# Masked attention with residual: the second batch's rows fetched later, its queries moved up, a slot formula with fewer dependent steps

## The chip, the core and the metric

The kernel runs on one core of one Trainium2 chip. The metric is the device time of one execution in microseconds (us); three timed runs gave 977.62, 977.0 and 977.0, a median of 977.0. A profiled execution of the same program took 974.4 us, of which the profile's span, from the first to the last instruction, is 972.7.

The core has engines that run side by side, each through its own instructions in order: TensorE (PE for matmuls, PEld for its weight loads), VectorE (DVE), ScalarE (ACT), GpSimd (POOL) and SyncE (SP). They wait for each other through semaphores. Transfers are issued by SP (plain ones) and POOL (gathers and scatters by an index) and carried by 16 DMA engines.

## The reference

16 sequences of 1024 tokens with 512 features and a 0/1 mask per token; 8 heads of 64. The query, the key and the value are all the same projection:

```python
xt = jnp.transpose(x, (0, 2, 1))
q = xt @ Wq.T
qh = q.reshape(B, T, NH, dk).transpose(0, 2, 1, 3)
scores = scale * jnp.einsum('bhqd,bhkd->bhqk', qh, qh)
cmask = mask[:, None, None, :]
rmask = mask[:, None, :, None]
logits = (scores * cmask + (1.0 - cmask) * NEG) * rmask
attn = jax.nn.softmax(logits, axis=-1)
ctx = jnp.einsum('bhqk,bhkd->bhqd', attn, qh)
ctx = ctx.transpose(0, 2, 1, 3).reshape(B, T, D)
out = ctx @ Wo.T
return x + jnp.transpose(out, (0, 2, 1))
```

A masked token's own row of logits is all zero, so its result is the same for all masked tokens of a sequence: the mean of q over all tokens. An active token attends to the active tokens of its sequence only.

## The kernel before

The kernel packs the active tokens. A token's **slot** is its rank among the active ones if it is active, and otherwise the number of active ones plus its rank among the others. The first 512, 528 or 544 slots of a batch (one batch is one sequence) are the ones that attention is computed for; batch 0 has 512, batch 1 has 544.

Start. `order` counts the active tokens per batch (eight matmuls) and ranks the batches by it; "batch 0" is a place in this order. `permute` picks a place's mask, `sources` finds which batch of the input it is: `base` (the number of its first row in `x_in`) and `first_row`, an integer in memory that SP reads (`source`, a register load) before it can address the batch's own features in `x_nat_in`. `slots` (line 244) gets the ranks `pr` by eight matmuls of the mask against a triangle and against ones, the total `pn` by eight more, and makes the slot from them on DVE; then the slot's number of 128 (`hi`) and place in it (`lo`). `hot` makes a one-hot table of `lo`, `index` turns it by eight small matmuls into `idx`, the row numbers in slot order. `gather` then fetches 128 rows (256 KB) at a time, by POOL. `warm(n)` issues n matmuls of 128x512 on constants, which compute nothing that is used, so that TensorE is kept busy.

Each gathered chunk is transposed on TensorE (`xt`), and split into an upper and a lower 16-bit part `xh`, `xl` (`xsplit`: ACT, then DVE). `query(b, e, g)` projects one of four 128-feature blocks e, one half g of the slots, by twelve matmuls. ACT copies the result to `q`, DVE zeroes what lies past the active tokens (`hr`), and `qsplit` makes `hl`, from which SP's four transfers per e spread `xx`, the operands of `scores`. `value` transposes q (batch 0) or multiplies xx by a constant (the others).

The mean. A batch's features are loaded once more, whole and untransposed (`load_half`: 256 KB, `load_all`: 512 KB), and summed along the tokens: on ACT (`sum_half`, a copy with an accumulator), or for the last four halves of batch 1 on DVE (line 462). The mean goes as an extra column behind the slots of `xh`, `xl` and through `query`; `mq` is what comes out. `extra` says which batch carries another's mean in column A + 1 (A slots) beside its own in column A: before, batch 1 carries batch 0's. `load_all` uses the buffers `xm`, of which there are two; batch 1's halves use those, `ub`, and four of `xi`.

Then come the batches one after the other (`run`, from line 1179). A batch has 18 slots of the plan, four per pair of heads p and two more. In a slot TensorE computes one group of `scores` for two blocks of keys; ACT takes four exponentials of it (line 793); `attend` (line 813) multiplies an earlier pair's exponentials with the values. Between these, `plan[(slot, half)]` puts the other work by hand: the transposes, queries and values of the next batch n, the index and gathers of the batch after that, the rest of the last batch's. `free[slot]` holds loads and sums. TensorE's order in this part is exactly the order in which the program issues; the other engines' orders are decided by a scheduler with priorities (`high_priority`) and fixed in the compiled program. `behind(i)` puts instructions behind instruction i in that order, and the argument `after` of a load makes the transfer wait for an instruction.

The lines that the change touches in this plan: the start from line 1099 on (`slots(0, 1)`, `warm(9)`, `hot(0)`), the loads at line 1128, `half1` (line 1140), batch 0's own plan at line 1233, and the loads of later batches at line 1259.

## Time and profile before

| | before |
|---|---|
| median of three timed runs | 977.0 us |
| profiled execution, whole | 974.4 us |
| its span | 972.7 us |
| TensorE, busy in the span | 936.1 us, 96% |
| VectorE | 718.3 us, 74% |
| ScalarE | 648.6 us, 67% |
| GpSimd | 304.8 us, 31% |
| mean granted TensorE clock | 0.996 |

A row of the profile in order of time has the start in us from the span's start, the duration, the engine, the line, the operation, what it writes and reads by the program's names, the shape, and how many in a row. What stands in brackets is the engine's idle time just before and what ended it. A table by stretches gives for each stretch its length, every engine's busy time with the number of instructions, the granted clock (1.00 is full), the mean busy share of the DMA engines and GB/s.

### The profile page before, as it was taken

How to read it: one execution, taken by the hardware profiler on the slowest of the kernel's cores; microseconds unless marked ns; L12 is line 12 of the kernel's file. 1: busy time of each engine (PE TensorE's matmuls, PEld its weight loads, DVE VectorE, ACT ScalarE, POOL GpSimd, SP SyncE). 2: the span in 40 equal slices, each digit the busy share in tenths (PEclk: the TensorE clock that was granted, in tenths of full speed). 3: DMA queues.
4: the chain of work that ended last, by engine and by line, in shares of the span. 5: the costliest groups of instructions: out<-in, count | busy, mean ns of one | idle time of the engine just before them, and what ended most of it. 6: DMA issues, size and time to landing. Idle time of an engine off the chain costs nothing.

```text
span 972.7 us, 22828 instructions
## 1 busy us (share of the span) xinstructions
PE 936.1 (96%) x8124; PEld 582.3 (60%) x8124; DVE 718.3 (74%) x2441; ACT 648.6 (67%) x1677; POOL 304.8 (31%) x309
## 2 busy tenths in 40 slices
PE   7788999999999999999999999999999999999997
PEld 4455656656666666666666666666666666565543
DVE  7767867777776777877687777886777788785563
ACT  5766766667667676676767678666767766565651
POOL 2101013033250432505234240332505135243452
PEclk9999999999999999999999999999999999999999
DMA  8736455557565676756657677655657857555552
GB/s 253 211 99 171 136 164 160 160 179 213 166 191 165 179 216 188 214 144 200 184 178 225 192 231 223 188 155 142 198 172 239 235 151 211 144 163 161 168 179 101
DMA packets 79144, 176.30 MB, mean 181 GB/s; under 512 B 14544, under 2 KB 22480, under 8 KB 79024
## 3 DMA queue, kind: packets, MB, share of 16 engines
q1 hardware_dynamic: 57968, 107.09, 39.2%
q0 software_dynamic: 21056, 67.68, 22.4%
q8 instruction: 66, 1.08, 0.5%
q14 instruction: 54, 0.44, 0.2%
HBM read 91.36 MB, written 33.91 MB: 129 GB/s over the span
## 4 chain that ended last, share of the span: by engine, by line
PE 82%; DVE 7%; DMA 4%; ACT 4%; issue 2%; SPq 1%; POOL 0%; POOLq 0%; DVEq 0%; ACTq 0%
PE pss L813 21%; PE pss L778 17%; PE pm L937 17%; PE pm L552 16%; ACT p L793 2%; PE pss L831 2%; DMA xx<-hl 2%; PE pm L524 2%; PE pss L724 1%; DMA xa<-x_in,idx 1%; PE pm L615 1%; DVE xl L483 1%; PE pss L937 1%; DVE xa L943 1%; PE pm L867 1%
## 5 line engine op out<-in xcount | busy, mean ns | idle before, releaser
L793 ACT ACTIVATE p<-pss,nm 128x528 f32<-128x528 f32 (+2 forms) x512 | 354.4, 703 | 103.5 <-PE pss L778 96.3
L813 PE MATMUL pss<-p,v 128*64 128x264 f32 (+2 forms) x2048 | 243.0, 390 | 0.0
L778 PE MATMUL pss<-xx 128*128 128x118 f16 (+17 forms) x1856 | 214.7, 289 | 3.6 <-ACT p L793 2.0
L1006 POOL DMA_INDIRECT y_out<-xa,idx x68 | 81.9, 1205 | 409.0 <-DVE nq L690 84.8
L813 PEld LDWEIGHTS pss<-p,v 128*64 128x64 f32 x2048 | 141.6, 137 | 86.1 <-issue 5.8
L778 PEld LDWEIGHTS <-xx 128*128 128x128 f16 (+1 forms) x1856 | 103.4, 96 | 85.0 <-issue 35.1
L552 PE MATMUL pm<-xh,wqh 128*128 128x264 f16 (+5 forms) x512 | 141.9, 277 | 3.7 <-DVE xl L483 1.8
L552 PE MATMUL pm<-xh,wql 128*128 128x264 f16 (+5 forms) x512 | 141.3, 276 | 0.0
L552 PE MATMUL pm<-xl,wqh 128*128 128x264 f16 (+5 forms) x512 | 141.1, 276 | 0.0
L552 PEld LDWEIGHTS <-wqh 128*128 128x128 f16 x1024 | 96.4, 97 | 33.0 <-issue 14.1
L422 POOL DMA_INDIRECT xa<-x_in,idx x68 | 72.8, 1071 | 127.8 <-DMA y_out<-xa,idx 43.7
L793 ACT ACTIVATION_READ_ACCUMULATOR p<-pss,nm 128x1 f32 x512 | 105.2, 205 | 0.0
L937 PE MATMUL pm<-woh,ch 128*128 128x512 f16 x240 | 91.1, 380 | 0.0
L937 PE MATMUL pm<-woh,cl 128*128 128x512 f16 x240 | 90.9, 379 | 0.0
L937 PE MATMUL pm<-wol,ch 128*128 128x512 f16 x240 | 90.9, 379 | 0.0
L556 ACT ACTIVATE q<-pm 128x264 f32<-128x264 f32 (+5 forms) x128 | 50.9, 397 | 44.2 <-PE pm L552 44.0
L619 ACT COPY v<-pm 128x512 f32<-128x512 f32 x64 | 37.5, 586 | 59.8 <-PE pm L615 56.6
L1006 POOL DMA_INDIRECT y_out<-xi,idx x60 | 64.3, 1071 | 36.6 <-PE pss L724 16.8
L943 DVE SCALAR_TENSOR_TENSOR xa<-pm,xa 128x512 f32<-128x512 f32 x61 | 41.6, 682 | 46.1 <-PE pm L937 45.6
L937 PEld LDWEIGHTS <-ch 128*128 128x128 f16 x480 | 44.8, 98 | 47.5 <-issue 4.1
L422 POOL DMA_INDIRECT xi<-x_in,idx x60 | 59.6, 993 | 21.2 <-issue 15.8
L836 ACT COPY c<-pss 128x528 f32<-128x528 f32 (+2 forms) x64 | 38.3, 598 | 41.9 <-PE pss L831 26.4
(231 smaller groups left out, 1489.1 us busy)
## 6 DMA issues: line engine op xcount, KB each, us to landing
xm<-x_nat_in SPq DMA_DIRECT2D x56, 512.0 KB
xx<-hl SPq DMA_DIRECT2D x208, 136.0 KB
rb<-rd SPq DMA_DIRECT2D x72, 132.0 KB
xx<-hl SPq DMA_DIRECT2D x48, 128.0 KB
pt<-c SPq DMA_DIRECT2D x36, 132.0 KB
pt<-p SPq DMA_DIRECT2D x36, 132.0 KB
rb<-rd SPq DMA_DIRECT2D x32, 136.0 KB
ub<-ud SPq DMA_DIRECT2D x16, 256.0 KB
```

Source lines behind the costliest of these rows:

```text
L422: dma = self.nc.gpsimd.indirect_dma_start(out=tile[:n], out_offset=None, in_=self.x, in_offset=bass.IndirectOffsetOnAxis(ap=idx, axis=0))
L524: self.pe = nc.tensor.transpose(pt[:, c, :], x[:n, c * P:(c + 1) * P], self.ident[:n, :n]).ins
L552: self.beat = nc.tensor.matmul(pq, lhsT=w[:, c, e * P:(e + 1) * P], rhs=xx[:, c, cols], start=(k == 0), stop=(k == 3 * DC - 1)).ins
L556: nc.scalar.activation(s["q"][:, e, cols], pq, AF.Copy, scale=1.0 / (SX * SW))
L619: nc.scalar.copy(v, pv)
L778: m = nc.tensor.matmul(flat[:, c0:c1], lhsT=w, rhs=x, start=banks[n] not in banks[:n], stop=banks[n] not in banks[n + 1:])
L793: e = nc.scalar.activation(t, flat[:, at:at + A], AF.Exp, bias=s["nm"][p // 2][:, p % 2 * 2 + k:p % 2 * 2 + k + 1], scale=SCALE, accum_out ...
L813: mm = nc.tensor.matmul(pav[k * DK:(k + 1) * DK, g], lhsT=s["v"][p][:, i, k * DK:(k + 1) * DK], rhs=ps[k, i][:, cols], start=(i == 3), sto ...
L836: self.context_out = nc.scalar.copy(c[:, :A].rearrange("p (g c) -> p g c", g=2), pav).ins
L937: mm = nc.tensor.matmul(po[:cols.stop - cols.start], lhsT=a[:, e, cols], rhs=w[:, e, :], start=(e == 0 and k == 0), stop=(e == DC - 1 and ...
L943: return self.nc.vector.scalar_tensor_tensor(x, po, 1.0 / (SX * SW), x, ALU.mult, ALU.add).ins
L1006: dma = self.nc.gpsimd.indirect_dma_start(out=self.out, out_offset=bass.IndirectOffsetOnAxis(ap=idx, axis=0), in_=x, in_offset=None)
```

## The change

The slots of batch 0 and of batch 1 come from a new function, `slots_of`; the other batches keep `slots`. With m the mask, it makes 1 - m, 2m - 1 and (token number) x (1 - m) from the mask alone, counts the total first and the ranks second, and takes slot = (2m - 1) x rank + (1 - m) x total + token number x (1 - m). The comparison table `kk_kept` holds 544 in place of 640 as its fifth bound, so that the shift of slots past 544 needs one operation.

```diff
+        for k, first in ((0, P), (4, C)):
+            nc.gpsimd.iota(self.kk_kept[:, k:k + 4], pattern=[[P, 4]], base=first, ...)
...
+        nc.vector.tensor_scalar(free, mb, -1.0, 1.0, ALU.mult, ALU.add)
+        nc.vector.tensor_scalar(sign, mb, 2.0, -1.0, ALU.mult, ALU.add)
+        nc.vector.tensor_tensor(put, self.tok, free, ALU.mult)
...
+        nc.vector.tensor_copy(n, pn)
+        nc.vector.scalar_tensor_tensor(base, free, n, put, ALU.mult, ALU.add)
+        nc.vector.tensor_tensor(slot, sign, pr, ALU.mult)
+        nc.vector.tensor_tensor(slot, slot, base, ALU.add)
+        nc.vector.tensor_tensor(ge, slot..., self.kk_kept..., ALU.is_ge)
+        nc.vector.scalar_tensor_tensor(far, ge[:, :, 4], float(5 * P - C), slot, ALU.mult, ALU.add)
+        nc.vector.tensor_reduce(hi, ge, AX.X, ALU.add)
+        nc.vector.scalar_tensor_tensor(self.lo[:, b], hi, -float(P), far, ALU.mult, ALU.add)
...
-            self.sources(0, 2)
-            self.slots(0, 1)
-        self.warm(9)
-        self.hot(0)
+            self.slots_of(0)
+            self.hot(0)
+            self.sources(0, 2)
+        self.warm(6)
```

The last four half loads of batch 0 are issued behind the third transposed chunk and not the first. Batch 1's eight half loads go; its features come as four whole loads in batch 0's slots 5, 8, 11 and 14, between batch 2's, all through the two `xm` buffers, each summed on ACT two slots after its load (batch 2's were summed four slots after). Its mean is carried by batch 2 and not by batch 1.

```diff
-            if k == 0:
+            if k == 2:
                 for i in range(DC, 2 * DC):
                     self.load_half(0, i, self.pe)
-                for i in range(DC):
-                    self.load_half(1, i, self.pe)
...
-        self.extra = {1: 0, B - 5: B - 4, B - 2: B - 1}
+        self.extra = {1: 0, 2: 1, B - 5: B - 4, B - 2: B - 1}
...
-                        at = 3 * c + (k if b else 4)
+                        at = 3 * c + k + (0 if b else 4)
...
-                if b == 0:
-                    for k in range(2 * DC):
-                        if k >= DC:
-                            free.setdefault(0, []).append(lambda k=k: half1(k))
-                        free.setdefault(3 + k // 2, []).append(L(self.sum_half, 1, k))
```

Batch 0's plan (x: transposes of batch 1, q(e, g): its queries, v: values, tv, tc: tails, pre, post, hot, index, take: mask, slots, one-hot table, index and gathers for batch 2 on):

```diff
-                                (3, 0): query(0, 3, 1) + value(0, 3) + pk(b, 1) + x[:1],
-                                (5, 0): x[1:2], (5, 1): x[2:3],
-                                (7, 0): x[3:] + tp(b, 1) + q(0, 0) + bt(b, 1), (8, 1): pre,
-                                (9, 0): q(0, 1), (9, 1): q(1, 0) + post, (11, 0): hot,
-                                (12, 0): q(1, 1) + tc(0) + v(0) + rng[:2], (12, 1): index, (13, 0): take[:3],
-                                (14, 0): tv(0) + q(2, 0) + rng[2:], (14, 1): v(1) + q(2, 1) + pk(n, 0),
-                                (16, 0): q(3, 0) + tp(n, 0) + take[3:], (16, 1): q(3, 1),
-                                (17, 0): bt(n, 0) + v(2) + tc(1) + [(0, L(self.means, n))]}
+                                (3, 0): query(0, 3, 1) + x[:1] + value(0, 3) + pk(b, 1), (4, 0): x[1:2],
+                                (5, 0): x[2:3], (5, 1): x[3:],
+                                (7, 0): tp(b, 1) + q(0, 0) + bt(b, 1) + q(0, 1), (8, 1): pre + q(1, 0),
+                                (9, 1): post, (11, 0): hot + q(1, 1),
+                                (12, 0): tc(0) + v(0) + rng[:2] + q(2, 0), (13, 1): index,
+                                (14, 0): tv(0) + q(2, 1) + rng[2:] + take[:3], (14, 1): v(1) + q(3, 0) + pk(n, 0),
+                                (16, 0): q(3, 1) + tp(n, 0) + take[3:], (16, 1): bt(n, 0),
+                                (17, 0): v(2) + tc(1) + [(0, L(self.means, n))]}
```

More of the change, by code (lines that the diff above doesn't have):

```diff
@@ L117, in setup @@
         self.kk = iota("kk", [P, NB - 1], [[P, NB - 1]], P, 0)
+        self.kk_kept = fixed("kk_kept", [P, NB - 1])
+        for k, first in ((0, P), (4, C)):
+            nc.gpsimd.iota(self.kk_kept[:, k:k + 4], pattern=[[P, 4]], base=first, channel_multiplier=0,
+                           allow_small_or_imprecise_dtypes=True)
         self.ionb = iota("ionb", [P, NB], [[1, NB]], 0, 0)
@@ L280, in slots, with slots_of @@
                                     self.tok.unsqueeze(2).broadcast_to([P, TB, NB]), ALU.mult)
+    def slots_of(self, b):
+        nc = self.nc
+        n = self.n[:, b:b + 1]
+        mb = self.act16[:, b]
+        whole, half = self.sb([P, 7, TB], F32, "c", 4), self.sb([P, TB, 2 * NB], F16, "c", 4)
+        free, sign, put, base, slot, hi, far = (whole[:, k] for k in range(7))
+        ge, oh = half[:, :, :NB - 1], half[:, :, NB:]
+        nc.vector.tensor_scalar(free, mb, -1.0, 1.0, ALU.mult, ALU.add)
+        nc.vector.tensor_scalar(sign, mb, 2.0, -1.0, ALU.mult, ALU.add)
+        nc.vector.tensor_tensor(put, self.tok, free, ALU.mult)
+        pn = self.pm([P, 1])
+        for j in range(TB):
+            nc.tensor.matmul(pn, lhsT=self.on16, rhs=mb[:, j:j + 1], start=(j == 0), stop=(j == TB - 1))
+        pr = self.pm([P, TB])
+        nc.tensor.matmul(pr, lhsT=self.tri, rhs=mb, start=True, stop=False)
+        for s in range(1, TB):
+            self.pe = nc.tensor.matmul(pr[:, s:], lhsT=self.on16, rhs=mb[:, :TB - s], start=False, stop=(s == TB - 1)).ins
+        nc.vector.tensor_copy(n, pn)
+        nc.vector.scalar_tensor_tensor(base, free, n, put, ALU.mult, ALU.add)
+        nc.vector.tensor_tensor(slot, sign, pr, ALU.mult)
+        nc.vector.tensor_tensor(slot, slot, base, ALU.add)
+        nc.vector.tensor_tensor(ge, slot.unsqueeze(2).broadcast_to([P, TB, NB - 1]),
+                                self.kk_kept.unsqueeze(1).broadcast_to([P, TB, NB - 1]), ALU.is_ge)
+        nc.vector.scalar_tensor_tensor(far, ge[:, :, 4], float(5 * P - C), slot, ALU.mult, ALU.add)
+        nc.vector.tensor_reduce(hi, ge, AX.X, ALU.add)
+        nc.vector.scalar_tensor_tensor(self.lo[:, b], hi, -float(P), far, ALU.mult, ALU.add)
+        nc.vector.tensor_tensor(oh, hi.unsqueeze(2).broadcast_to([P, TB, NB]),
+                                self.ionb.unsqueeze(1).broadcast_to([P, TB, NB]), ALU.is_equal)
+        nc.vector.tensor_tensor(self.oht[:, b], oh, self.tok.unsqueeze(2).broadcast_to([P, TB, NB]), ALU.mult)
     def facts(self, b0, b1):
@@ L450, in load_half @@
             self.source(b)
-        t = self.sb([P, C], F32, "p", 12)[:, :T // 2] if b == 0 else \
-            self.sb([P, T // 2], F32, *((("xm", 2), ("ub", 3), ("xi", 8), ("xi", 8))[k // 2]))
+        t = self.sb([P, C], F32, "p", 12)[:, :T // 2]
         src = self.x_nat[bass.ds(self.st[b]["row"], 1), c * P:(c + 1) * P, h * T // 2:(h + 1) * T // 2].rearrange("o p t -> (o p) t")
@@ L459, in sum_half @@
         with self.behind(*self.exp):
-            if b == 1 and k > 3:
-                with self.nc.allow_low_precision(reason="float32"):
-                    self.nc.vector.tensor_reduce(s["ms2"][:, k:k + 1], s["xm"][k], AX.X, ALU.add)
-                return
             self.nc.scalar.activation(s["xm"][k], s["xm"][k], AF.Copy, accum_out=s["ms2"][:, k:k + 1])
@@ L528, in xt @@
         if k == 4 and b:
-            if b == 2 or b > 2 and A < self.wide[b - 1] and b not in self.extra:
+            if b == 1 or b > 2 and A < self.wide[b - 1] and b not in self.extra:
+                at = A + (b > 1)
                 for t in (self.xh, self.xl):
-                    nc.gpsimd.memset(t[:, :, A + 1:A + 2], 0.0)
+                    nc.gpsimd.memset(t[:, :, at:at + 1], 0.0)
             for o, col in [(o, A + 1) for o in [self.extra.get(b)] if o is not None] + [(b, A)] * (b not in self.extra.values()):
@@ L1114, in run @@
                 self.active(1, 2)
-                self.slots(1, 2)
+                self.slots_of(1)
             for f in halves:
@@ L1138, in run @@
         g1 = [(0, L(self.gather, 1, j)) for j in range(5)]
-        def half1(k):
-            with self.behind(self.last_xx):
-                self.load_half(1, k, self.beat)
         def wide_rest(c):
```

## The prediction

> **What bounds the kernel now.** I read the page's first line, then three kinds of view: how the time splits by stretches, who TensorE waited for, and the first 95 us in order of time.

> ```profile
> span 972.7 us, 22828 instructions
> ...
> core 0: us, PE busy (x) PEld busy (x) DVE busy (x) ACT busy (x) POOL busy (x), PEclk, DMA share, GB/s
> 0.00:50.00 50.00, 36.15 (x263) 21.74 (x265) 37.84 (x139) 31.57 (x79) 11.91 (x35) 0.97 0.79 231
> 50.00:100.00 50.00, 43.97 (x380) 27.04 (x377) 34.26 (x139) 33.06 (x88) 4.82 (x7) 0.97 0.47 130
> 100.00:972.70 872.70, 855.98 (x7488) 533.56 (x7486) 646.23 (x2166) 583.93 (x1512) 288.09 (x267) 1.00 0.62 181
> 46.00:50.00 4.00, 4.00 (x20) 1.89 (x20) 3.89 (x12) 3.07 (x9) 0.00 (x0) 0.57 0.67 207
> 83.00:88.00 5.00, 5.00 (x26) 2.44 (x25) 4.45 (x14) 1.44 (x3) 0.00 (x0) 0.66 0.03 13
> ```

> TensorE is the bound: from 100 us on it is idle for 16.7 of 872.7 us. The first 100 us are another matter: 13.9 us idle before 50 and 6.0 us from there to 100, and in two stretches the granted clock is down: (1 - 0.57) x 4 = 1.7 us are lost at 46 to 50 and (1 - 0.66) x 5 = 1.7 us at 83 to 88, where TensorE counts as busy throughout. The change touches only these 100 us. What is saved there should come out at the end nearly whole, since the rest is TensorE work in an order that stays, with the same batches' queries, scores and projections. The waits that matter here (who waited for whom, total, times, longest):

> ```profile
> PE pm L201 <- DVE given L198: 3.7, 1, 3.7
> ...
> PE pm L615 <- DMA xx<-hl: 2.2, 2, 1.8
> ...
> PE pss L778 <- ACT p L793: 2.0, 2, 1.8
> PE pm L612 <- DVE q L559: 2.0, 1, 2.0
> ...
> PE pss L333 <- DVE oht L279: 1.5, 1, 1.5
> ```

> The first, for the mask itself, stands ahead of everything that the change edits and stays. The others are its field.

> **Term 1, the start: from the mask to the first rows.**

> ```profile
> 6.46 0.16 DVE L232 CAST first_row<-base 1x2 int32<-1x2 f32 x1
> 6.77 0.16 DVE L258 TENSOR_TENSOR sc<-tok,pm 128x8 f32<-128x8 f32 x1 [0.16 <-PE pm L252]
> 6.81 4.00 PE L372 MATMUL warm<-on 128*128 128x512 f16 x9
> 7.67 11.00 SPq L454 DMA_DIRECT2D p<-x_nat_in  x8
> 9.12 1.22 DVE L324 TENSOR_TENSOR tmp<-io,lo 128x1024 f16<-128x1024 f16 x1
> 10.60 0.41 PE L333 MATMUL pm<-oht,tmp 128*128 128x9 f16 x8
> 11.57 1.29 POOL L422 DMA_INDIRECT xa<-x_in,idx  x1 [8.02 <-DVE hr L348]
> ```

> From the counts (L258) to the one-hot rows (L324) the old formula takes 9.12 - 6.77 = 2.35 us: eight dependent small steps, the comparison, the reduction over it and lo, some 0.2 us each. In the new one the three steps on the mask alone run while TensorE still counts, and after the ranks only sign x rank, + base, the comparison, the reduction and lo follow: five steps instead of eleven, 2.35 x 5 / 11 = 1.1 us, and 0.1 for two rows of sources between them. The ranks now come after the total, 0.2 us later, so hot(0) starts near 8.2 instead of 9.12. The index matmuls wait for hot(0)'s end and for the warming matmuls; nine of these held them to 10.60, six (4.00 / 9 = 0.44 us each) are through near 9.5. So the first gather goes out 1.0 us earlier, near 10.6.

> Against it stands a move that the words of the change don't name: sources(0, 2) now follows the slots, and its first_row, which SP must read before it can address batch 0's own rows, is written after hot(0), near 9.8 instead of 6.46. The first four half loads thus go out near 10.9, not 7.67: 3.2 us later, on top of the gathers. Their sums stand on ACT ahead of the first split of gathered rows (three of the four ahead of the first xh, the fourth ahead of the second).

> ```profile
> 15.03 0.19 ACT L464 ACTIVATION_READ_ACCUMULATOR p<-p 128x1 f32 x1
> 15.68 1.26 POOL L422 DMA_INDIRECT xa<-x_in,idx  x1 [0.30 <-issue]
> 16.34 0.60 ACT L482 ACTIVATE xh<-pss 128x512 f16<-128x512 f32 x1 [1.12 <-PE pss L524]
> 21.30 0.66 PE L524 MATMUL pss<-ident,xa 128*128 128x128 f32 x4 [0.42 <-DMA xa<-x_in,idx]
> 22.00 0.60 ACT L482 ACTIVATE xh<-pss 128x512 f16<-128x512 f32 x1 [0.69 <-PE pm L315]
> 29.72 0.61 ACT L464 ACTIVATE p<-p 128x512 f32<-128x512 f32 x1
> ...
> DMA to landing us min/median/max: 3.5/5.0/5.6
> ```

> Now the four sums end at 15.2 and the first split starts at 16.3. With loads 3.2 us later the sums end near 18.4 if nothing else changes, and the third near 17.6: the first split would start 1.3 us late, and of this I let 0.8 us reach the queries, the rest lying under waits for the fourth gather; that is the low end, -0.8. The high end: everything follows the index (1.0), and the fourth gather, which took the longest landing (15.68 to 21.3, 5.6 us) beside the second four half loads and batch 1's four, lands in the shortest, 3.5, since these loads now come after the third transpose or much later: 1.0 + 2.1 = 3.1. Value taken: **0.8 us**, nearer the low end, since the ACT order is fixed in the program and the fourth gather was only 0.42 us of TensorE idle. [...]

> The two extra iotas are POOL work before 3.6 us, when POOL then sits idle 8.02 us: nothing, at most their 0.13 us each. The second four half loads of batch 0 move behind the third transpose (near 19 instead of 16.8); their first sum starts at 29.72, so some 8 us cover them, and without that cover ACT would wait for a landing.

> **Term 2, batch 1's rows at 40 us.**

> ```profile
> 39.62 1.96 SPq L454 DMA_DIRECT2D xi<-x_nat_in  x4
> 41.96 0.39 ACT L556 ACTIVATE q<-pm 128x258 f32<-128x258 f32 x1
> 42.24 0.69 DVE L462 TENSOR_REDUCE ms<-xi 128x1 f32<-128x512 f32 x1 [3.20 <-DMA xi<-x_nat_in]
> 43.80 0.69 DVE L462 TENSOR_REDUCE ms<-xi 128x1 f32<-128x512 f32 x1 [0.87 <-DMA xi<-x_nat_in]
> 44.74 0.33 PE L612 MATMUL pm<-ident,q 128*128 128x128 f32 x1 [2.01 <-DVE q L559]
> 45.34 2.08 PE L778 MATMUL pss<-xx 128*128 128x512 f16 x8
> ```

> VectorE, in order, stands still for 3.20 and 0.87 us for half loads that SP sends only at 39.62, after its twelve transfers of xx. Behind it wait the masking of q (ready at 42.35), TensorE's transposes (2.01 us) and the next scores. The change takes these four reductions and both waits away. What is late next: the scores at 45.34 also need the last exponential, which ACT, with one xh split now ahead of it, ends near 42.35 + 0.60 + some 0.7 = 43.65. So the scores start near 43.75: **1.6 us**. Bounds: 0.5 (ACT later by one more operation and a hop) to 2.0 (the whole gap).

> **Term 3, the clock behind that wait.** The drop at 46 to 50 follows these idle times; without the 2 us gap I expect none: **1.7 us**, bounds 0 and 1.7.

> **Term 4, 50 to 100 us: batch 1 moved up in batch 0's plan.** Transposes of batch 1 come at slots 3 to 5 instead of 3 to 7, its queries one to three slots earlier, the index of batch 2 and its gathers one slot later.

> ```profile
> 56.87 0.28 PE L552 MATMUL pm<-xh,wqh 128*128 128x272 f16 x1 [0.94 <-DVE xl L483]
> ...
> 76.56 5.80 DMA xx<-hl
> ...
> 82.50 0.36 PE L615 MATMUL pm<-two,xx 128*128 128x64 f16 x7 [1.83 <-DMA xx<-hl]
> ...
> L464 ACT ACTIVATE xm<-xm x6: 652/1058/1086, 38.1 to 90.4; 128x1024 f32<-128x1024 f32 x4, 128x512 f32<-128x512 f32 x2
> L464 ACT ACTIVATION_READ_ACCUMULATOR xm<-xm x6: 187/222/230, 38.7 to 91.3; 128x1 f32 x6
> ```

> What can go: 0.94 us for the splits ahead of the first query, 1.5 us for the one-hot rows of the index, 1.83 us for an xx that was sent at 76.6 amid the gathers and landed at 82.4, and the clock's second drop behind it, 1.7: 6.0 us in all. What comes: batch 1's 2 MB as four loads of 512 KB through the two xm buffers that batch 2's four use, and sums two slots after the load instead of four. ACT had four sums of 1.06 + 0.22 and four halves of 0.65 + 0.22, now eight whole ones: 8 x 1.28 - 4 x 1.28 - 4 x 0.87 = +1.6 us, beside 50 - 33.1 = 16.9 us of ACT idle in this stretch; VectorE loses 4 x 0.69. The share of DMA was 0.47 here, so there is room. Batch 1's mean goes into a column that batch 2's query multiplies already, so TensorE has no more to do; the few small VectorE copies of that column lie among batch 1's other work. Bounds: -4 (ACT's 1.6 and a 2.4 us hold of xx behind a load on SP, both on the path) to +6.0. Half of the possible is taken: **3.0 us**.

> **Sum:** 0.8 + 1.6 + 1.7 + 3.0 = 7.1 us, from the profiled execution's 974.4 us to 967.3. The median of the three timed runs is 977.0, 2.6 above that execution; I carry the offset: **969.9 us**.

> **Rivals.**

> ```profile
> 33.56 1.13 PE L778 MATMUL pss<-xx 128*128 128x512 f16 x6 [1.30 <-DMA xx<-hl]
> ...
> 38.33 1.57 PE L778 MATMUL pss<-xx 128*128 128x512 f16 x8 [1.79 <-ACT p L793]
> ...
> 91.89 1.71 PE L778 MATMUL pss<-xx 128*128 128x472 f16 x16
> ```

> Only half of it (973.7 us): the clock drops all the same, and batch 1's early queries fill one gap and open another. TensorE still stands 1.79 us for ACT ahead of 38.33, a wait that the change leaves, and a gap of 1.83 us was enough at 82. Against: that gap itself was not followed by a drop before. 0.8 + 1.6 + 0 + 0.9 = 3.3. [...]
> It doesn't do what it says (976.5 us, within 0.2%): the later loads on ACT's path take term 1 to 0, and ACT's 1.6 with a 1.2 us wait on SP take term 4 to -2.8: 0 + 1.6 + 1.7 - 2.8 = 0.5. For it: ACT's fixed order; against: the 2.01 us wait has no other cause left.
> All gaps close (964.6 us): the high ends of terms 1 and 4 at once, 3.1 + 1.6 + 1.7 + 6.0 = 12.4.
> Slower (981.9 us): the two xm buffers. Each of the last six loads may be sent only after the sum two loads before it; on SP, queries' xx transfers stand behind these loads, and on ACT the exponentials behind the sums. One of the 18 slots of batch 0's plan, which runs from its first scores to batch 1's, is (91.89 - 33.56) / 18 = 3.2 us, so a sum comes 6.5 us after its load was due. Two halves sent at 39.62 and 40.20 were in at 43.8: 4.2 us for 512 KB. The rival decides once a load takes more than 6.5 us from its due slot, 2.3 us of hold on SP. If each of the six then holds ACT, and TensorE behind it, 2 us: 12 - 7.1 = 4.9 us over. Against it: ACT's 16.9 us idle and a lightly used DMA.

> **How the numbers follow.** Forecast 0.62, half of it 0.17, nothing 0.09, all gaps 0.05, slower 0.07. A difference under 0.2% (2 us) can't be told from none here. Faster: 0.62 + 0.17 + 0.05 = 0.84; same 0.09; slower 0.07. The range: the sum of the high ends, 3.1 + 2.0 + 1.7 + 6.0 = 12.8, gives 964.2, less the 0.6 by which the timed runs differ 963.6 below; above it takes in half of it and nothing, to 977.0.

> **What would show it.** Step 1: first gather near 10.6, first half load near 10.9, first xh between 15.5 and 17.6, the fourth xh before 21.5. Step 2: no VectorE wait on x_nat_in, scores of the second pair near 43. Step 3: a granted clock of 1.00 from 44 to 50. Step 4: TensorE idle under 4 us from 50 to 100, no wait on xx over 1 us, ACT waiting on no xm load. It is wrong if ACT stands on a DMA of x_nat_in for more than a microsecond at a time, or if TensorE's idle time after 100 us grows by what was won before.

## The result, and the profile after

| | before | changed |
|---|---|---|
| median of ten runs, us | 977.0 (976.2 to 979.4) | 974.6 (971.2 to 976.3) |
| profiled execution, us | 974.4 | 975.2 |
| its span and mean granted clock | 972.7, 0.996 | 973.5, 0.994 |

The changed kernel takes 0.9971 of the time before (95% interval 0.9958 to 0.9983): 2.4 us faster, between 1.7 and 4.1. The forecast was 7.1 us faster. The sign is right, two thirds of the gain are missing, and the trace of the changed kernel is no shorter than that of before. In this trace the first TensorE matmul starts at 2.91 us, in that of before at 3.69, so 0.78 is to be added ahead of a comparison of points.

The split by stretches of the changed kernel (the columns as in the prediction):

```profile
0.00:50.00 50.00, 36.01 (x260) 22.15 (x262) 34.69 (x133) 28.46 (x69) 12.10 (x39) 0.93 0.65 187
50.00:100.00 50.00, 42.82 (x376) 26.66 (x373) 35.12 (x135) 37.16 (x97) 4.66 (x5) 0.97 0.59 174
100.00:973.50 873.50, 856.58 (x7491) 534.05 (x7489) 647.14 (x2172) 584.19 (x1514) 289.61 (x267) 1.00 0.62 181
```

Behind 100 us nothing has changed: 16.9 us idle there (16.7 before). Ahead of 50 us the clock is lower than before (0.93 against 0.97), and from 50 to 100 TensorE is idle for 7.2 us instead of 6.0. Now the start, rows of each engine's timeline. Below them stand the row of the DMA view for the gathers, which ends with the median from issue to landing (of the first three, 6.1 to 6.7), and TensorE's first transpose in the kernel before:

```profile
9.04 0.16 DVE L236 CAST first_row<-base 1x2 int32<-1x2 f32 x1
...
9.92 13.74 SPq L489 DMA_DIRECT2D p<-x_nat_in  x8
...
10.04 1.30 POOL L458 DMA_INDIRECT xa<-x_in,idx  x1 [6.23 <-DVE hr L384]
...
16.88 0.63 PE L555 MATMUL pss<-ident,xa 128*128 128x128 f32 x4 [2.75 <-DMA xa<-x_in,idx]
...
17.12 0.63 ACT L495 ACTIVATE p<-p 128x512 f32<-128x512 f32 x1 [2.26 <-DMA p<-x_nat_in]
...
17.75 0.58 ACT L513 ACTIVATE xh<-pss 128x512 f16<-128x512 f32 x1
```
```profile
xa<-x_in,idx POOLq DMA_INDIRECT x4, 6.7
```
```profile
15.70 0.60 PE L524 MATMUL pss<-ident,xa 128*128 128x128 f32 x4
```

The first gather does go out earlier (10.82 on the scale of before, where it was 11.57), and the half loads go out beside it, as forecast. But that gather now takes 6.7 us to land, where before it took 3.5, TensorE stands still for 2.75 us where it had no wait, and the first split starts at 18.53 on the scale of before instead of 16.34. ScalarE, too, stands still, 2.26 us for the third half load (2.46 and 3.27 in the traces of e5 and e12 below): the prediction named more than a microsecond of this as a sign of being wrong. The split follows that load's sum at once, and the transposed rows were ready only 0.2 us before it (0.1 and 0.8 there): the late gather and the late load would each alone have held it for about as long.

The clock is read best in the steps in which the trace has it: ahead of 100 us this trace has six changes of it, from 18.86 to 93.96, all whole multiples of 3.41 us apart. These are pairs of such steps of the changed kernel, the second of each pair being the one that follows (TensorE's busy time is the second number, the clock the third from the end):

```profile
15.45:18.86 3.41, 1.50 (x10) 1.03 (x11) 0.66 (x2) 1.74 (x5) 0.00 (x0) 1.00 0.75 293
18.86:22.28 3.42, 3.42 (x14) 2.11 (x13) 2.30 (x8) 1.27 (x3) 0.00 (x0) 0.50 0.03 8
32.52:35.93 3.41, 1.76 (x10) 0.88 (x10) 2.42 (x14) 2.24 (x9) 1.62 (x2) 1.00 0.95 261
35.93:39.34 3.41, 3.41 (x17) 1.79 (x17) 3.12 (x10) 2.12 (x6) 0.00 (x0) 0.50 1.08 273
87.13:90.54 3.41, 1.30 (x12) 0.94 (x10) 3.10 (x12) 2.88 (x10) 1.36 (x2) 1.00 0.93 358
90.54:93.96 3.42, 3.42 (x26) 1.79 (x25) 3.42 (x15) 0.79 (x2) 0.46 (x1) 0.50 0.92 254
73.48:76.89 3.41, 1.67 (x20) 1.19 (x19) 3.38 (x12) 3.41 (x12) 0.00 (x0) 1.00 0.51 161
76.89:80.30 3.41, 3.41 (x27) 1.99 (x27) 2.92 (x12) 3.41 (x10) 0.27 (x1) 1.00 0.82 193
```

Three steps are halved, behind steps in which TensorE was idle for 1.91, 1.65 and 2.11 us; each costs 1.7 us of clock (half of 3.41). The two halvings of before, at 46 and 83 us, are gone, and three others have come. A step with 1.74 us idle, at 73.48, was not followed by one.

The middle: the scores of the second pair, and waits of TensorE from 50 to 100 us (total, times, longest), and below them the wait for m in the kernel before.

```profile
45.47 0.66 PE L644 MATMUL pm<-ident,q 128*128 128x128 f32 x4 [0.62 <-ACT q L588]
...
46.86 0.66 PE L555 MATMUL pm<-ident,xa 128*128 128x128 f32 x4 [0.73 <-DVE xl L514]
47.35 1.56 PE L810 MATMUL pss<-xx 128*128 128x512 f16 x8
```
```profile
PE pss L717 <- DVE m L710: 4.0, 2, 2.1
...
PE pss L810 <- ACT p L825: 1.7, 1, 1.7
...
PE pm L899 <- DVE xl L514: 1.1, 1, 1.1
```
```profile
PE pss L685 <- DVE m L678: 0.7, 2, 0.5
```

The 2.01 us ahead of 44.74 are gone, with 0.73 in their place (the 0.62 ahead of it was 0.84 before). TensorE no longer waits for any xx behind 50 us; it waits instead twice for m, a maximum that VectorE takes of the scores, 4.0 us, where before it was 0.7.

### The profile page after: what moved, and what is told of

Its sections match the earlier page's. It is cut to its first block, busy times and chain, and to the rows that moved or that the text cites. A ratio compares the mean times of both kernels' runs of the same rounds, so it can differ in the third digit from the quotient of the medians.

```text
span 973.5 us, 22814 instructions
## 1 busy us (share of the span) xinstructions
PE 935.4 (96%) x8121; PEld 582.9 (60%) x8121; DVE 716.9 (74%) x2439; ACT 649.8 (67%) x1677; POOL 306.4 (31%) x311
## 4 chain that ended last, share of the span: by engine, by line
PE 81%; DVE 7%; ACT 5%; DMA 4%; issue 1%; SPq 0%; POOL 0%; POOLq 0%; DVEq 0%; ACTq 0%
PE pss L845 21%; PE pss L810 17%; PE pm L969 16%; PE pm L584 16%; ACT p L825 3%; PE pss L863 2%; PE pm L555 2%; PE pss L756 1%; DMA xa<-x_in,idx 1%; PE pm L647 1%; DVE xl L514 1%; DMA xm<-x_nat_in 1%; PE pss L969 1%; ACT xm L495 1%; DMA xx<-hl 1%
## 5 line engine op out<-in xcount | busy, mean ns | idle before, releaser
L969 PE MATMUL pm<-woh,ch 128*128 128x512 f16 x240 | 91.1, 380 | 0.0
L975 DVE SCALAR_TENSOR_TENSOR xa<-pm,xa 128x512 f32<-128x512 f32 x61 | 41.7, 683 | 45.8 <-PE pm L969 45.3
L458 POOL DMA_INDIRECT xi<-x_in,idx x60 | 59.4, 990 | 21.5 <-issue 15.8
L495 ACT ACTIVATE xm<-xm 128x1024 f32<-128x1024 f32 x60 | 64.0, 1070 | 0.4 <-DMA xm<-x_nat_in 0.4
```

The costliest lines, as they stand in the source:

```text
L458: dma = self.nc.gpsimd.indirect_dma_start(out=tile[:n], out_offset=None, in_=self.x, in_offset=bass.IndirectOffsetOnAxis(ap=idx, axis=0))
L495: self.nc.scalar.activation(s["xm"][k], s["xm"][k], AF.Copy, accum_out=s["ms2"][:, k:k + 1])
L969: mm = nc.tensor.matmul(po[:cols.stop - cols.start], lhsT=a[:, e, cols], rhs=w[:, e, :], start=(e == 0 and k == 0), stop=(e == DC - 1 and ...
L975: return self.nc.vector.scalar_tensor_tensor(x, po, 1.0 / (SX * SW), x, ALU.mult, ALU.add).ins
```

## The experiments

The kernels ran on several chips, on which the kernel before took 977 to 995 us, so ratios to the runs of before on the same chip are compared, not times. Three points are read from each trace, in us from the first matmul: the scores that wait for the first xx, and the first and the fourth attend (first matmul pss<-p,v of a group). "Halved" counts the halved steps ahead of 100 us.

| run | ratio to before (95%) | scores | 1st attend | 4th attend | 1st to 4th | halved |
|---|---|---|---|---|---|---|
| before (first trace) | 1 | 29.87 | 44.71 | 90.86 | 46.15 | 2 |
| e9_before_again | | 30.04 | 43.33 | 89.15 | 45.82 | 2 |
| e16_before_trace | | 30.44 | 43.75 | 92.48 | 48.73 | 1 |
| changed | 0.9971 (0.9958, 0.9983) | 32.56 | 46.52 | 92.14 | 45.62 | 3 |
| e5_changed_again | 0.9967 (0.9946, 0.9988) | 32.13 | 44.95 | 90.56 | 45.61 | 2 |
| e12_changed_beside | 0.9953 (0.9937, 0.9970) | 32.25 | 45.06 | 90.65 | 45.59 | 2 |
| e1_row_first | 0.9940 (0.9914, 0.9965) | 29.30 | 42.12 | 86.15 | 44.03 | 0 |
| e15_row_first_again | 0.9964 (0.9935, 0.9992) | 29.90 | 42.71 | 88.32 | 45.61 | 1 |
| e2_loads_late | 0.9940 (0.9911, 0.9969) | 31.00 | 43.81 | 87.92 | 44.11 | 0 |
| e10_two_loads | | 29.78 | 42.60 | 86.63 | 44.03 | 0 |
| e6_gap_filled | 0.9966 (0.9944, 0.9988) | 31.36 | 44.19 | 91.50 | 47.31 | 2 |
| e3_old_plan | 1.0004 (0.9978, 1.0030) | 32.63 | 44.49 | 93.91 | 49.42 | 3 |
| e4_slots_alone | 0.9983 (0.9959, 1.0007) | 29.61 | 42.80 | 91.28 | 48.48 | 1 |
| e13_rows_alone | 1.0000 (0.9976, 1.0024) | 30.47 | 42.34 | 93.26 | 50.92 | 2 |
| e14_rows_plan | 0.9951 (0.9924, 0.9979) | 30.45 | 44.41 | 90.05 | 45.64 | 2 |
| e7_row_first_cover | 0.9927 (0.9905, 0.9949) | 29.82 | 42.63 | 86.75 | 44.12 | 1 |
| e11_cover_again | 0.9896 (0.9870, 0.9922) | 29.62 | 42.43 | 85.02 | 42.59 | 0 |
| e8_row_first_cover_sums | 0.9939 (0.9917, 0.9960) | 29.38 | 43.34 | 86.39 | 43.05 | 1 |

**Where the loads stand at the start.** e1 writes the first row first, so that the loads go out ahead of the gathers; e2 sends them all behind the third transpose; e10 keeps only two of the first four beside the gathers; e5 and e12 are the changed kernel unaltered.

```diff
+            self.sources(0, 2)
             self.slots_of(0)
             self.hot(0)
-            self.sources(0, 2)
```

and e2 (in e10 the first loop stays with range(2), and the second begins at 2):

```diff
-        for i in range(DC):
-            self.load_half(0, i)
...
-                for i in range(DC, 2 * DC):
+                for i in range(2 * DC):
```

> The changed kernel, but the first row's number is written ahead of the first slots again, so that the first four half loads go out about 2.3 us ahead of the first gather instead of beside it. Theory A (the loads on top of the gathers made the first gather take 6.7 us instead of 3.5, left TensorE a gap of 2.75 us at 14 us, and that gap brought the clock fall at 19 to 22 us): first gather in by about 14.3 on the changed kernel's time scale, no gap over 1 us there, no fall before 35 us, first scores near 32.0 instead of 35.48, and about 971 us (969.5 to 972.5) against the changed kernel's 974.6. Rival B (the start is covered: what is won there is lost again at a wait before 50 us): first scores within 1 us of 35.5 and 974 to 975 us. Rival C (the clock falls come by chance of phase and not from that gap): the gap goes, a fall of 1.7 us still comes before 35 us, and about 973.

> The changed kernel, but all eight half loads of the first batch's rows go out behind the third transpose, so no load of rows stands beside the first three gathers, with the slots, the index and the first row left as they are. Theory A: the first gather takes 3.5 to 4 us from its issue (10.04) instead of 6.7 and is in by 14, the gap of 2.75 us goes, the first xh is no later than 15.5, and the whole is 971 to 972.5 us unless the sums, which then come some 10 us later on ScalarE, take it back. Rival D (the gathers are slow for another reason, such as the weights' loads that run at the same time): the first gather still takes over 6 us, and 974 to 975 us.

> The changed kernel with two of the first four half loads behind the third transpose, so that 512 KB instead of 1 MB go out beside the first gathers. Theory A (each half load beside the gathers costs them time): the first gather lands between 4.5 and 6 us after its issue instead of 6.7, the idle time ahead of the first transpose is 0.3 to 1.6 us instead of 2.0 to 2.75. Rival D (the gathers are slow for another reason): over 6 us and over 1.9 us as with four.

> The changed kernel itself, beside the variants that follow and on their chip. Theory A: the ratio to before stays within 0.996 to 1.000, the first gather again takes over 6 us, and at least one clock fall comes within 5 us behind the gap of 2 to 3 us ahead of the first transpose. Rival C (the falls come by chance, not from this gap): a gap of the same length and no fall before 35 us.

> The changed kernel beside the run before this one: 0.996 to 0.998 of before. Theory W: each halved step behind a step with TensorE idle over 1.6 us, the first one behind the gap ahead of the first transpose if 2 us of that gap lie in one step.

The first transpose of gathered rows, one row of TensorE's timeline each in e1, e2, e10 and e12:

```profile
15.58 0.63 PE L555 MATMUL pss<-ident,xa 128*128 128x128 f32 x4 [0.21 <-DMA xa<-x_in,idx]
```
```profile
16.27 0.60 PE L555 MATMUL pss<-ident,xa 128*128 128x128 f32 x4
```
```profile
15.24 0.63 PE L555 MATMUL pss<-ident,xa 128*128 128x128 f32 x4 [0.75 <-DMA xa<-x_in,idx]
```
```profile
16.82 0.63 PE L555 MATMUL pss<-ident,xa 128*128 128x128 f32 x4 [2.37 <-DMA xa<-x_in,idx]
```

With four half loads beside the gathers TensorE waits 2.04 to 2.75 us in four traces (the changed kernel's three and e3), with two 0.75, with the loads ahead 0.21 in e1 and 0.53 to 0.98 in e15, e7, e11 and e8. That e2 shows no wait says nothing, as there the 13 warming matmuls, slower in that trace (4.71 us; 2.97 in the changed kernel's), hold the transpose. The packets of the gathers' queue, which the traces keep, tell more: from its issue to the end of its packets the first gather takes 5.7 to 6.0 us with four half loads beside it (five traces), 4.4 with two, 4.1 to 4.6 with the loads ahead (e1, e15, e4, e7, e8, e11) and 3.3 with none (e2). So it is the loads, and theory A holds against D. In e1 no step ahead of 100 us is halved:

```profile
0.00:50.00 50.00, 36.86 (x289) 22.99 (x290) 36.23 (x136) 31.46 (x78) 12.05 (x39) 1.00 0.69 193
50.00:100.00 50.00, 42.64 (x386) 27.11 (x385) 38.64 (x145) 38.35 (x100) 4.65 (x5) 1.00 0.65 179
```

The scores in e1, e15 and e10 come 2.2 to 3.3 us earlier than in the changed kernel's traces, and 0.4 to 0.5 us earlier than before's on average (29.7 against 30.1). The timed runs don't resolve this: e1's ratio, 0.9940, lies ahead of the changed kernel's three (0.9953 to 0.9971), e15's, 0.9964, lies among them, and the intervals overlap.

**The clock's share.** e6 keeps the rows late and fills the wait with warming matmuls.

```diff
-        self.warm(13)
+        self.warm(22)
```

> The changed kernel with 22 warming matmuls instead of 13 ahead of the first transpose: nothing is loaded or gathered earlier, only TensorE is kept busy through most of the 2.75 us in which it waits for the first rows. It tells the clock's share of the loss at the start from the late rows' share. Theory A (the gap brings the fall at 19 to 22 us): no fall before 35 us, first scores some 1 to 1.7 us earlier from the first matmul than the changed kernel's 32.57 (35.48 - 2.91), and about 1.5 us (0.002) off the changed kernel's ratio, while the first transpose comes no earlier. Rival F (the rows alone set the first scores, the fall lay under other waits): same ratio within 0.0007 and first scores the same within 0.5 us.

Three steps of e6: the one ahead of the first transposes, and a pair later on.

```profile
14.83:18.24 3.41, 3.35 (x19) 1.70 (x18) 3.41 (x20) 2.29 (x7) 0.54 (x1) 1.00 0.84 306
...
55.81:59.22 3.41, 1.50 (x14) 1.05 (x13) 1.26 (x11) 3.04 (x10) 0.00 (x0) 1.00 0.29 114
59.22:62.63 3.41, 3.41 (x18) 2.22 (x16) 2.10 (x8) 0.56 (x2) 0.00 (x0) 0.50 0.60 192
```

The step at the start is now busy (3.35 of 3.41 us), no halving follows, and the scores come 0.8 to 1.2 us earlier than in the changed kernel's traces: that much of the loss at the start was the clock, the rest late rows. But the ratio did not move, 0.9966 beside e5's 0.9967, though with intervals of 0.002 either way a gain of 1 us would not show. In its trace the wait for m, as long as in the other traces, fell whole into one step (1.91 us idle), and the next one, from 59 us, is halved; the traces of the changed kernel, e5, e12, e1 and e2 have no halved step there. Theory A was right at its place; that the gain reaches the end is not shown.

**The plan.** e3 puts batch 0's plan of before back into the changed kernel; e4 puts the new slots alone (with six warming matmuls in place of nine) into before; e13, e14 and e15 build the change up from before on one chip: rows, rows and plan, everything but the row's late number.

> The changed kernel with the plan of batch 0 as before: queries, transposes and index of the following batches at their old slots; rows, slots and start as changed. Theory A (the move of the queries gained about as much as it gave back: ScalarE's whole-row sums ahead of the splits and exponentials, and no TensorE work between the top and the bottom of the first peak): between the attend at 48 us and the one at 95 us the changed kernel won only 0.5 us over before, so 975 us (974 to 976.3). Rival B (the moved queries won the 3 us that the forecast gave them, and something else lost it): 977 to 978 us. Rival E (the move lost): below 973.5 us.

> The kernel before with only the new formula for the slots and six warming matmuls instead of nine; rows, first row's number, plan and loads as before. Theory A (the new formula itself gives what it seems to: hot(0) 1.4 us earlier from the mask's arrival, the first gather 0.7 to 1.0 us earlier): 976.0 us (975.3 to 976.8) against 977.0. Rival B (the start is covered by the fourth gather): 977.0 within 0.5. Rival C (a clock fall is moved or spared): a whole 1.7 us off either of these.

> The kernel before with the second batch's rows alone changed (whole rows during batch 0, their mean through batch 2's column, sums on ScalarE); plan, start and slots as before. Theory T (the traces as they stand: the wait at 40 us cost TensorE 0.8 to 2.0 us in three traces, and ScalarE's sums give little back): 0.9985 of before (0.998 to 0.9995). Theory U (the timed runs are longer than the traces through the old plan's wait on xx at 80 us, 1.8 to 3.0 us in the traces, and the halved clock behind it): 0.999 to 1.001, since these stay.

> The run before this one with the new plan of batch 0 as well: rows and moved queries, start and slots as before. Theory T: the plan gives only 0.1 us apart from the clock, so 0.998 to 0.999. Theory U: no wait on xx over 1 us at 80 us, and 0.995 to 0.997 of before, 3 us from the plan; its timed runs then have a smaller spread than before's.

> All edits but the place of the first row's number, once more, as the last step of this ladder: against rows and plan it adds the new slots, six warming matmuls instead of nine and the second half loads behind the third transpose. Theory A: the first gather goes out 0.9 us earlier than in the run before this one and 0.5 to 1.5 us are won: 0.993 to 0.995 of before. Rival B (the start is covered): the same as the run before this one within 0.5 us.

> The kernel before once more for a third trace of it. Theory U: a wait on xx at 80 us of 1.8 to 3 us, a halved clock step behind it where over 1.9 us lie in one step, and if this execution is as long as the timed ones, the time beyond the first two traces stands there or at the wait for the second batch's rows at 40 us. Otherwise the place of the 3 us by which the timed runs are longer than the traces stays open.

> The kernel before, for its trace on the chip of the runs beside it. Theory W (the granted clock is set anew every 3.41 us on a grid that is fixed within a run, and is halved for one step where TensorE stood idle for some 1.7 to 2 us or more of the step before): steps of 3.41 us again, any halved step ahead of which TensorE was idle over 1.6 us, and no halving after a step with under 1.6 us. Rival C (falls come by chance): a halved step behind a busy one. For the plan: if the old plan's wait on xx at 80 to 90 us is 2.9 us here, as in the runs with the old plan on other chips, and not 1.83 us as in the first trace, then it is the chip and not the edits that makes the difference.

e16, the third trace of before, shows what the first two did not (SP's and POOL's issues, then TensorE), and below it the first trace and e13 at the same place:

```profile
85.61 0.47 SPq L586 DMA_DIRECT2D xx<-hl  x1
...
87.41 0.59 SPq L589 DMA_DIRECT2D xx<-hl  x1
...
86.44 0.96 POOL L422 DMA_INDIRECT xa<-x_in,idx  x1 [9.20 <-ACT p L793]
87.70 0.88 POOL L422 DMA_INDIRECT xt<-x_in,idx  x1 [0.30 <-issue]
...
91.91 0.53 PE L615 MATMUL pm<-two,xx 128*128 128x64 f16 x7 [3.05 <-DMA xx<-hl]
```
```profile
87.34 0.47 SPq L586 DMA_DIRECT2D xx<-hl  x1
...
89.66 0.94 POOL L422 DMA_INDIRECT xa<-x_in,idx  x1 [10.93 <-ACT p L793]
...
91.69 0.36 PE L615 MATMUL pm<-two,xx 128*128 128x64 f16 x7 [0.36 <-DMA xx<-hl]
```
```profile
89.95 0.21 PE L647 MATMUL pm<-two,xx 128*128 128x64 f16 x1 [2.82 <-DMA xx<-hl]
91.00 0.53 PE L647 MATMUL pm<-two,xx 128*128 128x64 f16 x7 [0.83 <-DMA xx<-hl]
```

With the old plan the second half of query 2 sends its xx amid the gathers of batch 2, and the values that need it come 3 us later. The old plan stands in six traces: four of them (e3, e4, e13, e16) have this wait, 2.82 to 3.05 us, and in e3, e4 and e16 a halved step begins at 89 to 92 us; two (before and e9) have it only as 0.36 and 0.39 us. What differs is the gather beside it. In the four, the first gather goes out 0.1 to 0.8 us behind the first of the xx transfers, and from that transfer to the last value that waits for them 6.2 to 6.5 us pass; in the two it goes out 2.3 us behind, and 4.35 us pass (87.34 to 91.69 here). That is 2 us of the difference. The rest is that TensorE asks some 0.7 us later there: in both a halved step (0.50 from 83.7 to 87.1 us in the first trace, from 81.9 to 85.4 in e9) had just slowed it. Neither was tried by itself. No trace with the new plan has it. From the first to the fourth attend the old plan takes 45.8 to 50.9 us (median 48.6), the new one 44.0 to 47.3 (nine traces without the covers below, median 45.6): 3.0 us. In the ladder the plan is the step that pays: 1.0000 with the rows alone, 0.9951 with the plan, then 0.9964 with the slots and the rest of the start (theory U; the intervals of the first two just touch, and the last two can't be told apart). e3, at 1.0004 against the changed kernel's 0.9953 to 0.9971, says the same from the other side: its rival B, the 3 us, held. The slots alone, 0.9983, may be 1.7 us or nothing.

The rows alone did what the forecast said at their place: against e16, with the scores at the same point (30.47 and 30.44), the first attend of e13 comes 1.4 us earlier. By the fourth it is 0.8 us later: the time won was given back there, where e13 has the old plan's wait and two halved steps.

**What the plan gave back.** e7 and e11 are e1 with a half query as cover at both waits for m, e8 adds later sums.

```diff
-                                (7, 0): tp(b, 1) + q(0, 0) + bt(b, 1) + q(0, 1), (8, 1): pre + q(1, 0),
+                                (7, 0): tp(b, 1) + q(0, 0) + q(0, 1) + bt(b, 1), (8, 1): pre + q(1, 0),
...
-                                (16, 0): q(3, 1) + tp(n, 0) + take[3:], (16, 1): bt(n, 0),
-                                (17, 0): v(2) + tc(1) + [(0, L(self.means, n))]}
+                                (16, 0): tp(n, 0) + take[3:], (16, 1): q(3, 1),
+                                (17, 0): bt(n, 0) + v(2) + tc(1) + [(0, L(self.means, n))]}
```

and for e8:

```diff
-                        free.setdefault(at + (2 if b + 2 in self.extra else 4), []).append(L(self.sum_half, x, c))
+                        free.setdefault(at + ((2 if b else 3) if b + 2 in self.extra else 4), []).append(L(self.sum_half, x, c))
```

> The first row's number written first, as in the run of that name, and in batch 0's plan one query's half put between the top and the bottom of a peak at both places where TensorE waited for VectorE's maximum m (1.90 us at 55 us and 2.11 us at 85 us there): the second half of query 0 ahead of the bottom in slot 7, the second half of query 3 between top and bottom in slots 16 and 17. Theory A (the moved queries gave back up to 4 us by taking TensorE's cover away from these two waits): both gaps under 0.6 us, 2 to 4 us faster than the run with the first row alone, whose ratio to before was 0.994. Rival G (the wait only moves on, to the exponentials behind the peak's bottom): the gaps shrink, others of the same size open within 8 us, and the ratio stays within 0.001 of 0.994.

> The run before this one with ScalarE's whole-row sums three slots behind their loads instead of two. Theory A (the sums, 1.28 us each in pairs ahead of splits and exponentials, made the waits of 1.05 us at 51 and 1.74 us at 71 us): these two shrink by 1 us or more together, 1 to 2.5 us faster than without it. Rival G (a sum must come somewhere on ScalarE, and the next load waits for its buffer): the waits move by a slot, no change within 0.7 us, or slower if a load comes late for the following sum.

> The run with the first row written first and the two covers once more, beside the changed kernel on one chip: 0.991 to 0.994 of before and 3 to 5 us ahead of the changed kernel, if the gain is the loads' place, the covers and fewer halvings; within 1.5 us of the changed kernel if the earlier ratio was the chip's luck.

The covers took the first wait from 1.90 to 0.50 us and the second from 2.11 to 1.56, so 1.4 us from the first to the fourth attend (44.03 to 42.59, both without a halved step): less than the 2 to 4 expected, since the second wait stays. e11, beside the changed kernel on one chip, is the fastest kernel here: 0.9896 against 0.9953, 967.7 us against 973.0 (e7, the same kernel on another chip, had 0.9927), and its four runs all had a mean clock of 0.999, where the changed kernel's went from 0.991 to 0.999. Its stretches:

```profile
0.00:50.00 50.00, 37.50 (x294) 23.47 (x294) 35.48 (x136) 32.28 (x79) 12.28 (x39) 1.00 0.68 193
50.00:100.00 50.00, 44.20 (x405) 28.19 (x405) 40.19 (x151) 39.72 (x104) 4.88 (x5) 1.00 0.63 179
```

e8 was a miss: the waits of 1.05 and 1.74 us stand as they were. Its ScalarE rows ahead of the second say why:

```profile
65.64 0.22 ACT L495 ACTIVATION_READ_ACCUMULATOR xm<-xm 128x1 f32 x1
66.88 0.40 ACT L588 ACTIVATE q<-pm 128x274 f32<-128x274 f32 x1 [1.03 <-PE pm L584]
68.29 0.69 ACT L825 ACTIVATE p<-pss,nm 128x512 f32<-128x512 f32 x1 [1.01 <-PE pss L810]
```

Two sums still stand there, but between them and the exponentials ScalarE waits twice for TensorE, so they were not late. From 68.29 on ScalarE is busy for 3.4 us and TensorE has 2.0 us of work to do meanwhile. Ahead of the 1.05 us a sum still stands too, and what makes that wait stays open.

## Why the prediction went wrong

**Term 1 is the step that failed: forecast +0.8 us with a low end of -0.8, traced -2.2** (scores at 32.3 on average in three traces, 30.1 before). The points themselves were foreseen: gather and half load together near 10.6 to 10.9 (10.82 and 10.70 on that scale). But the prediction priced the later loads only by ScalarE's order, the sums ahead of the first split, and let 0.8 us of it through; for the gathers it took the times of before, 3.5 to 5.6 us, as bounds, though none of those gathers had four half loads issued in the same 1.5 us. Beside them the first gather took 6.7, and the third load's sum, forecast to end near 17.6, ended at 18.63 on that scale (17.85 here). So the split came at 18.53 where 1.3 us late would have been 17.6, and TensorE's wait of 2.75 us, 1.91 of it in one step, had no term, nor had the halved step that followed. With the row's number first, the term is +0.5 in the traces of e1 and e15, 0.3 under the value taken.

**Term 2, +1.6:** right where it acts, 1.4 in the pair e13 and e16, and the VectorE wait on x_nat_in is gone. Alone it shows no gain at the end, 1.0000, though with 0.0024 either way 1.6 us are not excluded. The scores of the second pair were to come near 43 and came at 48.13 on that scale (47.35 here): of the 5.1 us between, 3.5 are term 1's in this trace and 1.7 the halved step at 36 us.

**Term 3, +1.7:** wrong. From 44 to 50 us the clock is 1.00 as forecast, but the halved steps ahead of 100 us are 3, 2 and 2 in the changed kernel's traces and 2, 2 and 1 in before's. The prediction took a halving as belonging to its gap. The gap of 2 us went (0.73 in its place), and others came: in the changed kernel's trace the halved steps stand behind 1.91, 1.65 and 2.11 us idle in one step, and the wait of 1.90 us for m, cut by a step's edge, has none behind it.

**Term 4, +3.0:** the size is that of the plans' medians (48.6 to 45.6; from before's own three traces, 46.9 on average, it is 1.3), by another way: of the wait on xx that the prediction read at 82.5, 1.83 us, the larger sister at 88 to 92 was missing from the trace that it had. TensorE idle from 50 to 100 was to be under 4 us and is 7.2, since the moved queries uncovered the two waits for m. ScalarE waits for no load there. SP does stand for the sums before it may load again, 6.5 us in all, but TensorE waits for no xx behind it: the slower rival, the two xm buffers, did not come.

With these, 7.1 - 3.0 (term 1) - 1.7 (term 3) = 2.4, which is the measured gain; but that it fits so well is in part luck. Term 1's loss already holds the halved step behind its gap, term 2 alone showed no gain at the end, and the timed runs do not resolve what term 1 cost there. In the traces themselves the gain does not appear: the changed kernel's three reach the fourth attend at 91.1 us on average, before's three at 90.8. Two of these three are short executions, though. The first, 974.4 us, is shorter than all ten timed runs of before, and e9, 972.9, shorter than all 17 on its chip (from 974.5), while e16, with the 3 us wait, took 992.9 where the median of its chip was 987.7. So the timed runs of before lie between; how many of them have the wait is not shown, as they leave no trace.

Of the rivals, half the gain (973.7 us) came nearest to the 974.6 measured, and its conditions came true: the clock drops all the same, and the early queries fill one gap and open another, the waits for m. But it, too, took 0.8 for term 1.

## What to carry to other kernels

When a step is moved, follow what it releases on other queues to the moment at which it now runs, and price how it and the transfers that it then meets slow each other, not only their order: here one small write behind one VectorE operation put 1 MB beside the gathers that start the kernel, and the first of them took 6.7 us to land where it had taken 3.5. A trace of one execution can lack a wait that others have (here two of before's three), so a second and third trace of the kernel before are worth more than a finer reading of the first. And cover a wait with work that is there anyway before moving that work away.

## What the hardware showed beside it

In these six traces a halved step follows steps with TensorE idle for 1.65, 1.91 and 2.11 us (changed), 1.83 and 2.01 (before), 1.69 and 2.02 (e9), 2.11 and 2.37 (e12), 1.91 and 2.12 (e6) and 3.23 (e16); none follows steps with 1.74 (changed), 1.79 (before), 1.63 (e9) and 1.79 (e12). So from 1.65 to 1.79 us idle both were seen, and what decides there stays open; of theory W it held in e9 and e12 that each halved step has over 1.6 us idle ahead of it. In e3 two halved steps follow each other (0.50 from 90 to 96 us).

One wait shows what its place in a step was worth. TensorE's first wait for m is 1.90 us long in the changed kernel's trace, where a step's edge at 59.82 cuts it into 1.34 and 0.56, and no halved step follows; in e6's it fell whole into one step (1.91 us idle), and the next is halved. The second wait for m, 2.11 us, fell whole into one step in the traces of the changed kernel, e12 and e6, each time with a halved step behind it; the trace of e1, with the same wait, has a clock of 1.00 from 50 to 100 us. So the wait that was cut cost its length, and a wait of this size that fell whole into one step its length and 1.7 us of clock (half of 3.41). The ten timed runs of the changed kernel differ by 5.1 us, largely with the clock: they run from 971.2 us at a mean clock of 0.999 to 976.3 at 0.995.
